# Picking table rows in quarters of 256 edges on 32 partitions instead of halves of 512 edges on 64

## The chip, the core and the metric

The kernel runs on one core of one Trainium2 chip. The core has TensorE (PE in the profile; its weight loads are shown apart as PEld), VectorE (DVE), ScalarE (ACT), GpSimd (POOL) and SyncE (SP), which issues most transfers. Each engine works through its own instructions in order and waits on semaphores of the others. The metric is the device time of one execution in microseconds, and the time of a kernel is the median of its runs.

## The reference

A graph layer with residual. There are 12500 nodes with 64 features and 212500 edges, sorted by `dst`; the inner layer calls `src` its `row` and `dst` its `col`.

```python
h = jnp.maximum(_layernorm(x, axis=-1), 0.0)
edge_in = jnp.concatenate([h[row], h[col], dist], axis=1)      # row = src, col = dst
e = jax.nn.silu(edge_in @ eW1 + eb1)                            # 129 -> 128
e = jax.nn.silu(e @ eW2 + eb2)                                  # 128 -> 128
agg = jax.ops.segment_sum(e, row, num_segments=h.shape[0])
node_in = jnp.concatenate([h, agg], axis=1)
out = jax.nn.silu(node_in @ nW1 + nb1) @ nW2 + nb2
x = x + out
```

The first product splits in three: `h[row] @ eW1[:64]`, `h[col] @ eW1[64:128]` and `dist * eW1[128]`. The kernel makes the first two per node and not per edge.

## The kernel before

Nodes are put in 100 buckets (node number modulo 100, 125 nodes each). Table `ta` holds `h @ eW1[:64]` and is used by `src`; table `tb` holds `h @ eW1[64:128]` and is used by `dst`. A short copy of the first rows of `tb`, called `tb0`, serves the first 30 blocks.

Work on edges has two parts, which are interleaved by hand.

**Sending.** The edges come in 208 blocks of 1024, two blocks to a pair, 104 pairs. For each edge the kernel makes the row `tb[dst] + dist * w1d + eb1` and writes it to a DRAM buffer `q`, at a place that belongs to the bucket of its `src`. Because the edges are sorted by `dst`, a stretch of 512 edges (a half) needs few rows of `tb`: 58 consecutive rows, the window, which SP loads into `win` (line 305). DVE compares the destinations, relative to the window, with the partition number and gets a one-hot matrix `pick` (line 338 for a pair, line 335 for a single block). Partitions 0 to 63 hold the first half of the block and 64 to 127 the second; in each, 58 rows are the one-hot, one holds the edge weights (SP writes it over, line 319) and one holds ones. `win` has the two windows on the same partitions, side by side in columns with zeros elsewhere, so one product of 128 partitions by 256 columns gives the rows of 128 edges of each half (line 389, four products to a block, each run by TensorE as two passes). ACT copies the products to `qs` (line 400) and adds the node's place (line 411). DVE counts each edge's rank in its bucket: a one-hot of the buckets (`oh`, line 339), a running sum along the edges in three pieces (line 350) and a product (line 356); TensorE picks the rank out (line 383) and DVE makes the address `to` (line 405). POOL then writes 128 rows at a time to `q` with an indirect transfer (line 418, eight to a block).

**Summing.** The 450 steps of the second part take four tiles of 128 rows of `q` each: find the node in the bucket (lines 494 and 499), add the row of `ta` (lines 508 and 514), silu (518), second product and silu (540, 546, 550), sum per node (527, 560), add to `aggT` (571). The node products (lines 232 to 244) follow for each four buckets at the end. Line 235 there is a product of 64 partitions, done twice, once for each half of the partitions.

The order on TensorE, VectorE, ScalarE and SP is the order of the Python program (`manual_schedule`). The list `turn` gives the order of a summing step; where it says `None`, pieces of the sending (three to a block) are put in, as many as the summing will need. A block is loaded two blocks ahead, and counted one block ahead, of its sending.

**The start.** POOL fills `zeros`, loads the weights, and copies the two rows `w1d` and `eb1` into the three `win` buffers, one small transfer for each row, column half and buffer (line 212), then fills three `xs` buffers (line 754). DVE fills the end of `srcR` (line 768), normalizes the first nodes (lines 587 to 599), computes the windows' first rows `lo` (lines 671 and 673), the relative destinations `rowsD` (675), and the buckets of the sources (692 to 695). SP loads the second part of `srcR` only after the fill of line 768. After that the first blocks are sent while the tables are made.

At the very end a flag tells whether every edge fitted its window and its places; if not, a general and slow branch does all sums again.

Of the kernel before, what the change touches and what calls it, by code (L numbers as in the profile page):

```python
# [40 lines left out]
WL = 58  # L41
STEP = 25
SPAN = 3 * STEP + WL
FEW = 12
HB = 64
BLK = 1024
HALF = BLK // 2
TB = BLK // P
PAIR = 2 * BLK
G = 4  # L50
# [22 lines left out]
def tile_gnn(ctx: ExitStack, tc: tile.TileContext, x, src, dst, ew, eW1, eb1, eW2, eb2, nW1, nb1, nW2, nb2, out):  # L73
# [10 lines left out]
    assert LEVELS[-1][1] == -(-E // BLK) and PAD < BLK and PAD % FEW == 0 and (-PAD) % HALF >= FEW  # L84
# [83 lines left out]
    nc.vector.tensor_scalar(plus, part, HB - 0.5, None, op0=OP.is_gt)  # L168
    nc.vector.scalar_tensor_tensor(same, plus, -float(HB), part, op0=OP.mult, op1=OP.add)
# [11 lines left out]
    dests = dram.tile([NP, 2, 2, HALF], BF16, name="dests")  # L181
    bucks = dram.tile([NP, 2, BLK], BF16, name="bucks")

    tb0 = dram.tile([P * NE, H], F32, name="tb0")
# [21 lines left out]
    for win in wins:  # L206
        nc.vector.memset(win, 0.0)
        for a in range(2):
            for i, row in enumerate((w1d, eb1b)):
                at = a * HB + WL + i  # L210
                for g in range(2):
                    nc.gpsimd.dma_start(win[at : at + 1, g, a, :], row[:1, :])
# [42 lines left out]
    with ExitStack() as work:  # L255
# [18 lines left out]
        def load_rows(s):  # L274

            if s < nblocks:
                p, g = s // 2, s % 2
                if g == 0:
                    bc = ld.tile([P, 2, HALF], BF16, name="bc")
                    bb = ld.tile([P, 2, BLK], BF16, name="bb")  # L280
                    lists[p] = [bc, bb, None]
                bc, bb, _ = lists[p]
                if g == 0 or p == 0:
                    m = 1 if p == 0 else 2
                    r, r2 = dests[p, 0, g], bucks[p, g]
                    of = bass.AP(tensor=r.tensor, offset=r.offset, ap=[[BLK, 2], [0, HB], [1, m * HALF]])
                    nc.sync.dma_start(bc[:, g : g + m].rearrange("p g e -> p (g e)"), of)
                    of = bass.AP(tensor=r2.tensor, offset=r2.offset, ap=[[0, 112], [1, m * BLK]])
                    nc.sync.dma_start(bb[:112, g : g + m].rearrange("p g e -> p (g e)"), of)
                blk[s] = [bc[:, g], bb[:, g]]  # L290

        def load(s):

            if s < nblocks:
                p, g = s // 2, s % 2
                win = wins[p % NW]
                table, end = (tb0, NE * P) if s < EARLY else (tb, NB * P)
                assert s < EARLY or len(done_b) == NB // G
                if g == 0:
                    at = nc.sync.value_load(base_i[:, p : p + 1], min_val=0, max_val=end - SPAN)  # L300
                    for a in range(2):
                        rows = table[bass.ds(at, SPAN), :]
                        of = [[H, WL], [2 * STEP * H, 2], [1, H]]
                        of = bass.AP(tensor=rows.tensor, offset=rows.offset + a * STEP * H, ap=of)
                        nc.sync.dma_start(win[a * HB : a * HB + WL, :, a, :], of)
                    lists[p][2] = ld.tile([P, 2, HALF], F32, name="pick")
                blk[s] += [win[:, g], lists[p][2][:, g]]
            load_rows(s + 1)

        def weights(s):  # L310

            if s < nblocks:
                p, g = s // 2, s % 2
                pick = lists[p][2][:, g]
                e0 = s * BLK
                m = 1 if p == 0 or e0 + 2 * BLK > E else 2
                if m == 2 or e0 + BLK <= E:
                    of = bass.AP(tensor=ew.tensor, offset=ew.offset + e0, ap=[[HALF, 2], [BLK, m], [1, HALF]])
                    nc.sync.dma_start(lists[p][2][WL::HB, g : g + m, :], of)
                else:  # L320
                    for a in range(2):
                        m = min(HALF, E - e0 - a * HALF)
                        if m > 0:
                            of = bass.AP(tensor=ew.tensor, offset=ew.offset + e0 + a * HALF, ap=[[m, 1], [1, m]])
                            nc.sync.dma_start(pick[a * HB + WL : a * HB + WL + 1, :m], of)
# [49 lines left out]
        def send(s):  # L375
# [10 lines left out]
            two = [2 if G + t < nt else 1 for t in range(min(G, nt))]  # L386
            qps = [mm.tile([P, 2, 2, H], F32, name="qp", tag="mm") for _ in range(2)]
            for t, k in enumerate(two):
                nc.tensor.matmul(  # L389
                    qps[t // 2][:, t % 2, :k], pick[:, t * P : (t + 1) * P], win[:, :k], start=True, stop=True  # L390
                )
            parts = []
            for i, qp in enumerate(qps):
                qs = qsp.tile([P, 2, 2, W], F32, name="qs")
                mine = [(t, k) for t, k in enumerate(two) if t // 2 == i]
                same = [(slice(0, 2), 2)] if mine == [(2 * i, 2), (2 * i + 1, 2)] else [
                    (slice(t % 2, t % 2 + 1), k) for t, k in mine
                ]
                for ts, k in same:
                    nc.scalar.copy(qs[:, ts, :k, :H], qp[:, ts, :k, :])  # L400
                parts.append((i, same, qs))
            for i, same, qs in parts:
# [5 lines left out]
                places = locE[:, g * TB : (g + 1) * TB, p].rearrange("p (a i t) -> p i t a", a=2, i=2)  # L408
# [3 lines left out]
                for a in range(2):  # L412
                    for t in range(2 * i, 2 * i + 2):
                        j = a * G + t
                        if j >= nt:
# [5 lines left out]
                            in_=qs[:k, t % 2, a, :],  # L421
# [191 lines left out]
        def first_rows(g):  # L613
# [6 lines left out]
            nc.scalar.dma_start(tb0.rearrange("(p j) f -> p j f", j=NE)[:, g : g + G, :], got)  # L620
# [43 lines left out]
        def destinations():  # L664

            nc.scalar.copy(f, dstR)
            lim = lp.tile([NP, 1], F32, name="lim")
            nc.vector.tensor_scalar(lim, part[:NP], EARLY / 2 - 0.5, float((NB - NE) * P), op0=OP.is_gt, op1=OP.mult)
            nc.vector.tensor_scalar(lim, lim, float(NE * P - SPAN), None, op0=OP.add)
            yield  # L670
            nc.vector.tensor_scalar(lo[:, 0:1], fv[:, 0, 0:1], lim, None, op0=OP.min)
            for h in range(1, 4):
                nc.vector.tensor_scalar(lo[:, h : h + 1], lo[:, 0:1], float(h * STEP), None, op0=OP.add)
            for g in range(2):
                nc.vector.tensor_tensor(
                    rowsD[:, :, g, :],
                    fv[:, 2 * g : 2 * g + 2, :],
                    lo[:, 2 * g : 2 * g + 2, None].to_broadcast([NP, 2, HALF]),
                    op=OP.subtract,
                )  # L680
            nc.sync.dma_start(dests, rowsD)
            yield
            lot = mm.tile([1, NP], F32, name="lot", tag="mm")
            nc.tensor.transpose(lot, lo[:, 0:1], ident[:NP, :NP])
# [37 lines left out]
        def checks():  # L722

            ends = lp.tile([NP, 2, 4], F32, name="ends")
# [33 lines left out]
        with tc.tile_pool(name="lists", bufs=1, side="right") as lp:  # L758
# [5 lines left out]
            fv = f.rearrange("p (g e) -> p g e", e=HALF)  # L764
            lo = lp.tile([NP, 4], F32, name="lo")
            rowsD = lp.tile([NP, 2, 2, HALF], BF16, name="rowsD")
# [228 lines left out]
```

## Time and profile before

| | |
|---|---|
| median of 6 runs | 3200.42 us (3171.43 to 3207.57) |
| profiled execution | 3207.37 us, span 3205.6 us |
| PE busy | 2454.3 us (77%) |
| PEld busy | 2176.4 us (68%) |
| DVE busy | 1888.7 us (59%) |
| ACT busy | 1097.1 us (34%) |
| POOL busy | 1726.7 us (54%) |
| mean granted clock of TensorE | 0.859 |
| moved by the DMA engines | 495.01 MB |

In a group line of the profile stand the line of the kernel, the engine, the operation, what it writes and reads, the shapes, the count, then busy time and mean length of one in ns, then the engine's idle time just before and what ended it. A matmul's record runs on past the start of the next one, so the mean of one is longer than the distance between two. A timeline line has the start in us, the length of the merged stretch in us, the engine, the line, the operation and the count; "idle before" and what ended it stand in brackets. A line of windows has the stretch, its length, then the busy time (and count) of each engine, the granted clock, the DMA share and GB/s.

### The profile page before, as it was taken

The page shows a single profiled execution, that of the slowest core. Times are in us where ns is not written, and L with a number is a line of the kernel's source. Part 1 is how long each engine was busy: PE and PEld are TensorE (multiplying, and loading weights), DVE is VectorE, ACT ScalarE, POOL GpSimd, SP SyncE. Part 2 cuts the span into 40 slices and gives each one's busy share as a digit, 9 for nine tenths or more (in the row PEclk, how much of TensorE's full clock was granted, in tenths as well). Part 3 has the DMA queues.
Part 4 walks back from the last instruction along what each step waited for, and adds up shares of the span by engine and source line. Part 5 has one row for each costly group of instructions (what it writes and reads, how often), then busy time and mean ns, then how long its engine had stood idle before and what let it go on. Part 6 is the DMA issues. An engine that isn't in the chain of part 4 may idle for free. (4 is left out here: it accounts for less than half of the span.)

```text
span 3205.6 us, 48057 instructions
## 1 busy us (share of the span) xinstructions
PE 2454.3 (77%) x17253; PEld 2176.4 (68%) x17253; DVE 1888.7 (59%) x3129; ACT 1097.1 (34%) x2410; POOL 1726.7 (54%) x1737
## 2 busy tenths in 40 slices
PE   3563576655788888888888788878878888888998
PEld 2442465554677777777777777767767777788987
DVE  6554565655665656666566666666666666665433
ACT  3331232222233333333333333333333333344443
POOL 4566655666656656555565656556555555543000
PEclk9666777777798888898888989899899989899999
DMA  4553355555566656544444444444344444555441
GB/s 120 182 173 128 118 158 175 182 170 166 186 193 195 204 186 199 175 152 147 137 134 150 134 146 153 138 147 154 128 149 144 151 143 125 165 168 168 139 141 56
DMA packets 230686, 495.01 MB, mean 154 GB/s; under 512 B 43137, under 2 KB 85106, under 8 KB 230235
## 3 DMA queue, kind: packets, MB, share of 16 engines
q1 hardware_dynamic: 155454, 324.52, 32.5%
q0 software_dynamic: 54400, 123.05, 11.0%
q10 hardware_dynamic: 20586, 44.30, 4.7%
q8 instruction: 139, 2.28, 0.3%
q14 instruction: 107, 0.87, 0.1%
HBM read 305.41 MB, written 186.28 MB: 153 GB/s over the span
## 5 line engine op out<-in xcount | busy, mean ns | idle before, releaser
L418 POOL DMA_INDIRECT q<-qs,to x1661 | 1681.7, 1012 | 1230.2 <-ACT qs L411 674.8
L350 DVE TENSOR_TENSOR_SCAN misc<-oh,misc 100x342 f32<-100x342 f16 (+1 forms) x617 | 575.5, 933 | 207.3 <-remote 123.1
L518 ACT ACTIVATE e<-pt 128x512 f32<-128x512 f32 x450 | 270.6, 601 | 1205.3 <-remote 428.8
L560 PE MATMUL seg<-one,e 128*128 128x125 f32 x3600 | 547.8, 293 | 137.1 <-issue 95.9
L499 DVE TENSOR_SCALAR oneT<-lr,part 125x512 f32<-125x512 f32 x450 | 336.1, 747 | 472.2 <-remote 184.0
L560 PEld LDWEIGHTS seg<-one,e 128*128 128x128 f32 x3600 | 492.3, 207 | 155.9 <-issue 135.2
L546 PE MATMUL p<-w,e 128*128 128x128 f32 x3600 | 543.2, 294 | 51.4 <-issue 44.2
L546 PEld LDWEIGHTS p<-w,e 128*128 128x128 f32 x3600 | 509.6, 207 | 100.0 <-issue 66.5
L514 PE MATMUL pt<-oneT,a 125*128 125x256 f32 (+1 forms) x2200 | 532.8, 373 | 31.5 <-issue 30.4
L389 PE MATMUL qp<-win,pick 128*128 128x256 f32 x1664 | 491.0, 441 | 62.0 <-issue 42.3
L389 PEld LDWEIGHTS qp<-win,pick 128*128 128x128 f32 x1664 | 356.6, 224 | 134.3 <-issue 71.2
L514 PEld LDWEIGHTS pt<-oneT,a 125*128 125x128 f32 x2200 | 378.5, 212 | 66.0 <-issue 41.3
L571 DVE TENSOR_TENSOR aggT<-aggT,seg 128x500 f32<-128x500 f32 x250 | 168.0, 672 | 402.4 <-remote 140.9
L400 ACT COPY qs<-qp 128x512 f32<-128x512 f32 x418 | 233.4, 587 | 441.0 <-PE qp L389 108.5
L550 ACT ACTIVATE e<-p 128x512 f32<-128x512 f32 x450 | 271.2, 603 | 280.5 <-PE pt L514 67.7
L508 PE MATMUL pt<-ident,qt 128*128 128x128 f32 x1800 | 308.3, 296 | 61.6 <-ACT e L518 34.7
L356 DVE TENSOR_TENSOR own<-misc,oh 100x342 f16<-100x342 f32 (+1 forms) x623 | 319.5, 513 | 21.5
L527 DVE TENSOR_TENSOR one<-nodes,qt 128x500 f32<-128x500 f32 x450 | 301.4, 670 | 0.5 <-PE seg L560 0.5
L494 PE MATMUL lr<-identb,qt 128*125 128x128 bf16 x1800 | 202.4, 232 | 97.2 <-issue 68.0
L508 PEld LDWEIGHTS pt<-ident,qt 128*128 128x128 f32 x1800 | 214.3, 152 | 82.5 <-ACT e L518 42.6
L540 ACT COPY p<-b2f 128x512 f32<-128x512 f32 x450 | 269.3, 598 | 0.1
L494 PEld LDWEIGHTS <-qt 128*125 128x125 bf16 x1800 | 177.8, 146 | 119.5 <-issue 107.1
(120 smaller groups left out, 981.4 us busy)
## 6 DMA issues: line engine op xcount, KB each, us to landing
qt<-q SPq DMA_DIRECT2D x175, 576.0 KB
a<-ta SPq DMA_DIRECT2D x275, 256.0 KB
bb<-bucks SPq DMA_DIRECT2D x103, 448.0 KB
qt<-q SPq DMA_DIRECT2D x100, 288.0 KB
q<-qs,to POOLq DMA_INDIRECT x1661
bc<-dests SPq DMA_DIRECT2D x103, 256.0 KB
q<-zeros ACTq DMA_DIRECT2D x20, 1080.0 KB
q<-zeros ACTq DMA_DIRECT2D x10, 1440.0 KB
```

The costliest lines, as they stand in the source:

```text
L350: nc.vector.tensor_tensor_scan(run[:, :m], oh[:, cols], nil.to_broadcast([NB, m]), carry[-1] if carry else -1.0 - MID, op0=OP.add, op1=OP.add)
L356: nc.vector.tensor_tensor(own[:, cols], run[:, :m], oh[:, cols], op=OP.mult)
L389: nc.tensor.matmul(qps[t // 2][:, t % 2, :k], pick[:, t * P : (t + 1) * P], win[:, :k], start=True, stop=True)
L418: ins = nc.gpsimd.indirect_dma_start(out=q[:], out_offset=bass.IndirectOffsetOnAxis(ap=to[:k, j : j + 1], axis=0), in_=qs[:k, t % 2, a, :] ...
L494: nc.tensor.matmul(lr[:L, t, :], loc[:, at : at + 1].to_broadcast([P, L]), identb, start=True, stop=True)
L499: nc.vector.tensor_scalar(oneT, st[k].pop("lr")[:L], part1[:L, :], None, op0=OP.is_equal)
L508: nc.tensor.matmul(pt[:, t, :], qt[:, j, :H], ident, is_transpose=True, start=t == 0, stop=False, skip_group_check=True)
L514: nc.tensor.matmul(pt[:, cols, :], a[:L, b, :], oneT[:, cols, :], start=False, stop=True, skip_group_check=True)
L527: nc.vector.tensor_tensor(one.rearrange("p (b j) l -> p b j l", j=n), nodes1[:, None, None, :].to_broadcast(wide), loc[:, tiles[0][1] : ti ...
L546: nc.tensor.matmul(p2[:, t, :], e1[:, t, :], w2, start=False, stop=t == G - 1, skip_group_check=True)
L550: nc.scalar.activation(e2, p2, AF.Silu)
L560: nc.tensor.matmul(item[2][:, b, :], e2[:, t, :], one[:, t, :], start=j < G, stop=j >= G * (n - 1))
```

## The change

A block is divided in quarters of 256 edges instead of halves of 512. A quarter has 32 partitions: 30 rows of `tb`, one weight row, one row of ones. The four windows of a block start 15 rows apart. `pick` becomes 128 by 256 for a block, where it was 128 by 512. The product takes 64 partitions (two quarters, side by side in 256 columns as the halves were) and alternates between partitions 0 to 63 and 64 to 127; there are still four products to a block, of the same 256 columns. `win` is loaded by four transfers of 30 rows for each of two blocks, where there were two of 58. The eight tiles of a block are numbered so that a quarter is two tiles.

The windows' common start of a pair becomes the least over its eight quarters of first destination minus offset, bounded below; so that a window may start before row 0, `tb0` gets 16 rows of zeros in front. The offsets (0, 15, ..., 105) come from a new iota on POOL, `steps_i`, which DVE copies to `steps15`; in the program these stand just before the fill of `srcR`. The small transfers of `w1d` and `eb1` into the `win` buffers become 48, from 24. The counts by running sums along the edges, which the change's title names, are the same in both kernels.

```diff
-WL = 58
-STEP = 25
-SPAN = 3 * STEP + WL
+WL = 30
+STEP = 15
+SPAN = 7 * STEP + WL
+FRONT = 16
...
-HB = 64
+NQR = 4
...
-HALF = BLK // 2
+QR = BLK // NQR
...
-    tb0 = dram.tile([P * NE, H], F32, name="tb0")
+    tb0 = dram.tile([FRONT + P * NE, H], F32, name="tb0")
+    nc.gpsimd.dma_start(tb0[:FRONT], zeros[:FRONT, :H])
...
-        for a in range(2):
+        for a in range(NQR):
             for i, row in enumerate((w1d, eb1b)):
-                at = a * HB + WL + i
+                at = a * 32 + WL + i
                 for g in range(2):
-                    nc.gpsimd.dma_start(win[at : at + 1, g, a, :], row[:1, :])
+                    nc.gpsimd.dma_start(win[at : at + 1, g, a % 2, :], row[:1, :])
...
-                    of = bass.AP(tensor=r.tensor, offset=r.offset, ap=[[BLK, 2], [0, HB], [1, m * HALF]])
+                    of = bass.AP(tensor=r.tensor, offset=r.offset, ap=[[2 * QR, NQR], [0, 32], [1, m * QR]])
...
-                    for a in range(2):
-                        rows = table[bass.ds(at, SPAN), :]
-                        of = [[H, WL], [2 * STEP * H, 2], [1, H]]
+                    for a in range(NQR):
+                        rows = table[bass.ds(at - front, SPAN), :]
+                        of = [[H, WL], [NQR * STEP * H, 2], [1, H]]
                         of = bass.AP(tensor=rows.tensor, offset=rows.offset + a * STEP * H, ap=of)
-                        nc.sync.dma_start(win[a * HB : a * HB + WL, :, a, :], of)
-                    lists[p][2] = ld.tile([P, 2, HALF], F32, name="pick")
+                        nc.sync.dma_start(win[a * 32 : a * 32 + WL, :, a % 2, :], of)
+                    lists[p][2] = ld.tile([P, 2, QR], F32, name="pick")
...
-            two = [2 if G + t < nt else 1 for t in range(min(G, nt))]
+            halves = [[sum(4 * i + 2 * a + t < nt for a in range(2)) for t in range(2)] for i in range(2)]
             qps = [mm.tile([P, 2, 2, H], F32, name="qp", tag="mm") for _ in range(2)]
-            for t, k in enumerate(two):
-                nc.tensor.matmul(
-                    qps[t // 2][:, t % 2, :k], pick[:, t * P : (t + 1) * P], win[:, :k], start=True, stop=True
-                )
+            for t in range(2):
+                for i, n_of in enumerate(halves):
+                    if n_of[t]:
+                        at = slice(64 * i, 64 * i + 64)
+                        nc.tensor.matmul(
+                            qps[i][:, t, : n_of[t]], pick[at, t * P : (t + 1) * P], win[at, : n_of[t]], start=True, stop=True
+                        )
...
+            far = lp.tile([NP, 1], F32, name="far")
+            for h in range(-(-LAST // QR), 2 * NQR):
+                nc.vector.tensor_scalar(far, part[:NP], NP - 1.5, float(BEYOND), op0=OP.is_gt, op1=OP.mult)
+                assert h == 2 * NQR - 1
+                nc.vector.tensor_scalar(fv[:, h, :], fv[:, h, :], far, None, op0=OP.add)
...
-            nc.vector.tensor_scalar(lo[:, 0:1], fv[:, 0, 0:1], lim, None, op0=OP.min)
-            for h in range(1, 4):
-                nc.vector.tensor_scalar(lo[:, h : h + 1], lo[:, 0:1], float(h * STEP), None, op0=OP.add)
+            base = lp.tile([NP, 1], F32, name="base")
+            nc.vector.tensor_tensor(lo, fv[:, :, 0], steps15[:NP], op=OP.subtract)
+            nc.vector.tensor_reduce(base, lo, AX.X, OP.min)
+            nc.vector.tensor_scalar(base, base, lim, low, op0=OP.min, op1=OP.max)
+            nc.vector.tensor_scalar(lo, steps15[:NP], base, None, op0=OP.add)
...
+            steps15 = lp.tile([P, 2 * NQR], F32, name="steps15")
+            steps_i = lp.tile([P, 2 * NQR], I32, name="steps_i")
+            nc.gpsimd.iota(steps_i, pattern=[[STEP, 2 * NQR]], base=0, channel_multiplier=0)
+            nc.vector.tensor_copy(steps15, steps_i)
```

## The prediction

> **What bounds the kernel now.** I read the totals first, then the work by stage, then TensorE's own order around the product that the change touches, and last the start. The page: its first line, TensorE's busy tenths and its granted clock.
>
> ```profile
> PE 2454.3 (77%) x17253; PEld 2176.4 (68%) x17253; DVE 1888.7 (59%) x3129; ACT 1097.1 (34%) x2410; POOL 1726.7 (54%) x1737
> ...
> PE   3563576655788888888888788878878888888998
> ...
> PEclk9666777777798888898888989899899989899999
> ```
>
> TensorE is the fullest engine from about 800 us on (eight to nine tenths), and its clock there is near full. Before that it is half idle and slow. The same by stage, for line 389 alone (the product that changes):
>
> ```profile
> 0.00:340.00 340.00, 79.01 (x184) 52.93 (x184) 0.72 0.47 147
> 340.00:800.00 460.00, 88.22 (x280) 63.48 (x280) 0.74 0.53 165
> 800.00:2945.00 2145.00, 323.80 (x1200) 240.23 (x1200) 0.89 0.49 157
> ```
>
> Eight passes are a block: 23, 35 and 150 blocks. What TensorE waited for between 800 and 2800 us:
>
> ```profile
> PE misc L383 <- DVE own L356: 54.7, 34, 3.3
> PE seg L560 <- issue: 46.6, 67, 5.7
> ...
> PE seg L560 <- DVE aggT L571: 29.3, 26, 2.8
> ```
>
> These are small against 2000 us, so TensorE's own work sets most of the pace there. How one block stands in TensorE's timeline, and the only products on 64 partitions in the summing loop, those of line 235:
>
> ```profile
> 2002.06 1.06 PE L546 MATMUL p<-w,e 128*128 128x128 f32 x8
> 2002.95 1.89 PE L389 MATMUL qp<-win,pick 128*128 128x256 f32 x8
> 2004.68 1.05 PE L560 MATMUL seg<-one,e 128*128 128x125 f32 x8
> ```
>
> ```profile
> 2980.93 1.01 PE L232 MATMUL z<-aggT,w1g 128*128 128x250 f32 x4
> 2981.88 0.69 PE L235 MATMUL z<-hrn,w1n 64*128 64x250 f32 x4
> 2982.50 1.16 PE L546 MATMUL p<-w,e 128*128 128x128 f32 x8
> 2983.49 0.77 PE L241 MATMUL o<-w2n,zs 128*125 128x64 f32 x6
> ```
>
> Read the distances between starts. Line 389: 2004.68 - 2002.95 = 1.73 us for 8 passes, 0.216 each. Line 235: 0.62 us for 4 passes of 250 columns, where line 232 needs 0.95 for 4 passes of the same columns: the two halves overlap. The start, on POOL and DVE:
>
> ```profile
> 18.29 0.98 POOL L212 DMA_DIRECT2D win<-w1d  x2
> ...
> 22.12 2.41 POOL L212 DMA_DIRECT2D win<-w1d  x2
> ...
> 31.98 2.11 POOL L754 MEMSET xs<- 128x768 f32 x3
> ```
>
> ```profile
> 10.03 1.22 DVE L587 TENSOR_REDUCE mean<-x 128x16 f32<-128x1024 f32 x1 [6.71 <-DMA x<-in_x_dram]
> ...
> 19.23 0.21 DVE L671 TENSOR_SCALAR lo<-f,lim 104x1 f32<-104x1 f32 x1 [2.17 <-ACT f L666]
> ...
> 21.94 1.23 DVE L692 TENSOR_SCALAR t<-sf 104x2048 f32<-104x2048 f32 x1
> ```
>
> DVE starts on the nodes at 10 us; POOL is done with its small transfers and fills at 34 us and nobody waits for that.
>
> **The change part by part.** The sum is made against the profiled execution, 3207.4 us; the median shown is 7.0 lower, and I take that off at the end.
>
> *The products.* A pass of 250 columns costs 0.216 x 250/256 = 0.211. From line 232 to 235: 0.95 - 4 x 0.211 = 0.105 too much; line 235 to 546: 0.62 - 2 x 0.211 = 0.20 too much if two passes run side by side; after it line 546 takes 0.99 where an undisturbed one takes 0.89 (2002.06 to 2002.95), 0.10 too much. So a change to 64 partitions and back costs 0.405 us, and the passes in between run in pairs. A block then takes 4 x 0.216 + 0.405 = 1.27 instead of 1.73: 0.46 less at full clock. Over the run: the busy time has an overhang of 1.89 - 1.73 = 0.16 a block. For 340 to 800 us, 88.2 - 35 x 0.16 = 82.6, half is 41.3. At half clock the switch lies between 0.405 and 0.81; at a mean clock of 0.74 I take 0.50, 35 x 0.50 = 17.5, net 23.8. For 800 to 2945 us, 323.8 - 24.0 = 299.8, half 149.9, switches at clock 0.89 150 x 0.45 = 67.5, net 82.4. How much of this reaches the end? TensorE is busy 82% of the late stage and its waits for others are under a tenth; I take three quarters, 62 us. In the earlier stage (busy 63%, half clock much of the time) 0.55, 13 us. Ends: a quarter of both (27) and all (106). Before 340 us TensorE is half idle: 0 to 10, I take 3.
>
> The Trainium skill bears on this twice. "TensorE: Matmul & The Clock Gate", Part 3, gives a pack of row tiles the time of one matmul plus about 4 ns for each further tile; by that alone the gain of TensorE would be 41.3 + 149.9 = 191 us. "TensorEngine Tiling (Array Packing)", Key Properties, speaks against it: a change of tiling mode drains TensorE. The 0.405 us of the rows agrees with the second, and the sum goes by the rows.
>
> *The pick.* A pair's comparison shrinks from 128x1024 to 128x512:
>
> ```profile
> L338 DVE TENSOR_SCALAR pick<-bc,same,plus 128x1024 f32<-128x1024 bf16 x102 | 82.6, 809 | 0.0
> ...
> L335 DVE TENSOR_SCALAR pick<-bc,same,plus 128x512 f32<-128x512 bf16 x4 | 2.2, 544 | 9.0 <-DMA bc<-dests 9.0
> ```
>
> 102 x (0.809 - 0.544) = 27 us of DVE, which is idle two fifths of the time and mostly waits for TensorE. I take a tenth, 3 us; ends 0 and 14.
>
> *The start.* In the built order of the changed kernel the iota of the offsets stands on POOL behind 48 small transfers and the three fills, and DVE's copy of it stands ahead of the fill of `srcR` and of the first reduction over the nodes. So DVE, and behind it all of the start, waits for POOL. POOL reaches the first small transfer at 18.3 + 0.5 (the zeros of `tb0`). 48 at 0.48 (0.98 for two) end at 41.8; with the slower ones (13.7 us for 24 before) at 46.2. Fills 2.1, iota 0.2 (the length of line 136's): 44 to 48.5. Then copy and fill 0.7, reduction at 45 instead of 10.0: +35. Destinations were late before (DVE stood 2.17 us for `f`); that wait is gone, but the new step on `f` stands before the node's last two operations (1.5 us), and seven small DVE operations of about 0.15 replace four. I get line 692's successor at about 58 instead of 21.9, +36. SP's second part of `srcR` also starts only then, and ACT needs it seven us later; if it is late, up to 5 more. Two more window loads before the first product add 0.7. I take +37, ends 34 and 45. Everything after hangs on this chain, so it is paid in full.
>
> *SP.* 206 more window loads at 0.37 (the one at 2000.16 us) are 76 us of issue; SP stands 921 us waiting for DVE at line 469 between 800 and 2800, and a window is loaded two blocks ahead. Without that cover it would be 0.7 us a pair. The destinations' broadcast halves, about 13 of 495 MB. Both zero, ends 0 and +10. The 8 indirect transfers, the copies and the counts of a block stay.
>
> *The clock.* It is 0.74 where TensorE is 63% busy and 0.89 where it is 82%. Less work on TensorE takes it from 82% to about 80%: by that slope 0.015 of clock, 20 us or so; since it is work and not waiting that goes away, I take 10; ends 0 and 23.
>
> Sum: 3207.4 + 37 - 62 - 13 - 3 - 3 + 10 = 3173, less 7.0: 3166 us.
>
> **The rivals.**
> 1. *The loop keeps little.* TensorE arrives earlier only to stand at lines 383, 560 or 494, for the scans of DVE or for the "issue" waits that no engine ends. For: POOL (1228.8 us) and DVE (1339.8 us) work 8 to 9 us a block between 800 and 2945, out of 14; against: most DVE waits end on TensorE. At a third, 35 us with the rest: 3207 + 37 - 35 - 7 = 3202.
> 2. *The other side: the halves do not overlap.* Passes would follow each other, and the switches come on top: 85 us of TensorE, three quarters of it 64. 3207 + 37 + 64 - 7 = 3301. It decides as soon as a block takes more than its old 1.73 us. Against it: the 0.62 us of line 235.
> 3. *All of it reaches the end*, the clock holds: with 10 us from before 340 us and 5 from DVE, 3207 + 36 - 106 - 10 - 5 - 7 = 3115.
> That the windows of 30 are too narrow and the general branch runs, I rule out: counted over the reference's edge list, no destination lies more than 21 rows after its window's start.
>
> **How the numbers follow.** Forecast 0.50 (3145 to 3190), rival 1 0.22, rival 2 0.10, rival 3 0.18. The range 3115 to 3230 leaves out rival 2 and the low edge of rival 3. Half a per cent, 16 us, is about what the runs can tell. Faster (below 3184): 0.45 of the forecast, 0.03 of rival 1, all 0.18 of rival 3, 0.66. Same: 0.04 and 0.12, 0.16. Slower: 0.01, 0.07 and 0.10, 0.18.
>
> **What would show it.** The start: DVE's reduction over the first nodes at 43 to 48 us, ended by POOL. The product: eight passes with 1.2 to 1.3 us from first start to the next line's start, the records in pairs. The late stage: the same number of blocks in some 60 us less, clock 0.87 or more. I am wrong if a block still takes 1.7 us, if POOL's small transfers do not hold DVE, or if TensorE's idle time from 800 us on grows by as much as its work shrinks.

## The result, and the profile after

The changed kernel takes 3233.88 us (median of 20 runs, 3210.61 to 3256.62) where the kernel before takes 3201.81 (46 runs): a ratio of 1.0113, 95% interval 1.0093 to 1.0134. By the ratio it is about 36 us slower; the medians differ by 32 us. The profiled execution took 3235.39 us, with a span of 3233.6. All ratios here are over fast runs alone, so they need not be the quotient of the two medians, and the microseconds given with a ratio are the ratio's.

First the page: the totals, TensorE's busy tenths and its granted clock.

```profile
PE 2419.2 (75%) x17251; PEld 2070.9 (64%) x17251; DVE 1868.2 (58%) x3136; ACT 1088.4 (34%) x2406; POOL 1732.5 (54%) x1763
...
PE   1454377566588778778787888788788888888998
...
PEclk9655577666788888888988888899888988989999
```

TensorE has 35 us less busy time than before, and this execution's span is 28 us longer. The mean clock is 0.835, where it was 0.859. Only the first slices of the PE row differ plainly from before: the start is emptier.

The start, DVE in the timeline (start and length in us, in brackets the idle time before and what ended it):

```profile
41.76 0.17 DVE L786 CAST steps<-steps_i 128x8 f32<-128x8 int32 x1 [37.66 <-POOL steps_i L785]
42.08 0.47 DVE L789 MEMSET srcR<- 8x492 int32 x1
42.58 1.22 DVE L594 TENSOR_REDUCE mean<-x 128x16 f32<-128x1024 f32 x1
...
55.23 1.22 DVE L709 TENSOR_SCALAR t<-sf 104x2048 f32<-104x2048 f32 x1
```

DVE waits 37.66 us for POOL, whose iota follows the 48 small transfers. The line that makes `t` (692 before, 709 now) starts at 55.23 us instead of 21.94: +33.3. The 48 end at 39.5 us: none of them is slow as two pairs of before were.

The product, in TensorE's timeline:

```profile
2001.09 1.05 PE L567 MATMUL seg<-one,e 128*128 128x125 f32 x8
2002.07 1.13 PE L397 MATMUL qp<-win,pick 64*128 64x256 f32 x8
2003.14 0.44 PE L501 MATMUL lr<-identb,qt 128*125 128x128 bf16 x4
```

Eight passes now take 2003.14 - 2002.07 = 1.07 us, where they took 1.73. The line behind them is longer too, as these rows of the changed kernel in its later run on another chip show:

```profile
1503.96 1.14 PE L397 MATMUL qp<-win,pick 64*128 64x256 f32 x8
1505.03 1.16 PE L553 MATMUL p<-w,e 128*128 128x128 f32 x8
1506.02 1.05 PE L567 MATMUL seg<-one,e 128*128 128x125 f32 x8
```

Line 553 takes 1506.02 - 1505.03 = 0.99 us here, where line 546 took 0.89 undisturbed (2002.06 to 2002.95 in the prediction's rows). In the records at full clock lines 553 and 567 take 0.10 us more right behind the product than elsewhere, and lines 501 and 515 take 0.05.

Line 397 alone by stage (length, busy time and count of PE, then of PEld, clock, DMA share, GB/s):

```profile
340.00:800.00 460.00, 64.29 (x272) 35.37 (x272) 0.69 0.50 156
800.00:2945.00 2145.00, 216.31 (x1216) 123.37 (x1216) 0.88 0.48 154
```

Its busy time fell by 107.5 us in the late stage, with two blocks more in it. Now all engines in that stage, before and then after (PE, PEld, DVE, ACT, POOL):

```profile
800.00:2945.00 2145.00, 1753.30 (x12512) 1577.51 (x12512) 1339.78 (x2215) 772.79 (x1668) 1228.84 (x1209) 0.89 0.49 157
```

```profile
800.00:2945.00 2145.00, 1725.27 (x12431) 1488.09 (x12428) 1330.26 (x2225) 762.59 (x1657) 1238.24 (x1222) 0.88 0.48 154
```

Here is the whole case: 107.5 us left the product, but TensorE's busy time fell by only 28.0, for nearly the same work (12431 matmuls, 12512 before). The other 79.5 us came back in the other products, which became longer. Groups of the whole run show it, before and then after:

```profile
L560 PE MATMUL seg<-one,e 128*128 128x125 f32 x3600 | 547.8, 293 | 137.1 <-issue 95.9
...
L546 PE MATMUL p<-w,e 128*128 128x128 f32 x3600 | 543.2, 294 | 51.4 <-issue 44.2
```

```profile
L567 PE MATMUL seg<-one,e 128*128 128x125 f32 x3600 | 567.2, 301 | 128.9 <-issue 74.9
L553 PE MATMUL p<-w,e 128*128 128x128 f32 x3600 | 580.8, 304 | 97.1 <-issue 85.1
```

Lines that the change does not touch got 19.4 and 37.6 us longer (in the late stage alone 7.1 and 24.5), and one of them waits 45.7 us more. Lined up by block, POOL's first write of a block is late by 30.9 us in block 0, 33.0 in block 20, 51.1 in block 101, 32.6 in block 188 and 32.4 in block 206; the last step ends 33.3 us later. What follows the last step is 5.3 us shorter, for which no reason is shown. In this pair of executions the loop as a whole kept nothing, and the loss is the start. One pair settles that only roughly: executions of the kernel before differ by up to 58 us (3171.43 to 3229.45), and the lateness swings by some 19 us within this one. The experiments have to show it.

### The profile page after: what moved, and what is told of

Same layout as the page of the kernel before. It is cut to its first block, busy times and chain, and to the rows that moved or that the text cites. A ratio compares the mean times of both kernels' runs of the same rounds, so it can differ in the third digit from the quotient of the medians.

```text
span 3233.6 us, 48796 instructions
## 1 busy us (share of the span) xinstructions
PE 2419.2 (75%) x17251; PEld 2070.9 (64%) x17251; DVE 1868.2 (58%) x3136; ACT 1088.4 (34%) x2406; POOL 1732.5 (54%) x1763
## 2 busy tenths in 40 slices
DMA packets 238983, 481.91 MB, mean 149 GB/s; under 512 B 50165, under 2 KB 106996, under 8 KB 238526
## 3 DMA queue, kind: packets, MB, share of 16 engines
q0 software_dynamic: 55200, 123.07, 10.7%
## 5 line engine op out<-in xcount | busy, mean ns | idle before, releaser
L567 PE MATMUL seg<-one,e 128*128 128x125 f32 x3600 | 567.2, 301 | 128.9 <-issue 74.9
L553 PE MATMUL p<-w,e 128*128 128x128 f32 x3600 | 580.8, 304 | 97.1 <-issue 85.1
L553 PEld LDWEIGHTS p<-w,e 128*128 128x128 f32 x3600 | 530.9, 215 | 167.7 <-issue 128.2
L567 PEld LDWEIGHTS seg<-one,e 128*128 128x128 f32 x3600 | 502.7, 212 | 171.8 <-issue 147.9
L521 PE MATMUL pt<-oneT,a 125*128 125x256 f32 (+1 forms) x2200 | 549.5, 382 | 33.9 <-issue 32.9
L521 PEld LDWEIGHTS pt<-oneT,a 125*128 125x128 f32 x2200 | 391.1, 220 | 70.6 <-issue 45.8
L397 PE MATMUL qp<-win,pick 64*128 64x256 f32 x1662 | 328.3, 469 | 70.9 <-issue 54.0
L515 PE MATMUL pt<-ident,qt 128*128 128x128 f32 x1800 | 321.5, 305 | 70.0 <-ACT e L525 31.9
L407 ACT COPY qs<-qp 128x512 f32<-128x512 f32 x416 | 225.0, 590 | 392.5 <-remote 145.9
L397 PEld LDWEIGHTS qp<-win,pick 64*128 64x128 f32 x1662 | 187.5, 219 | 143.9 <-issue 107.1
```

What stands on the lines that cost most here:

```text
L397: nc.tensor.matmul(qps[i][:, t, : n_of[t]], pick[at, t * P : (t + 1) * P], win[at, : n_of[t]], start=True, stop=True)
L515: nc.tensor.matmul(pt[:, t, :], qt[:, j, :H], ident, is_transpose=True, start=t == 0, stop=False, skip_group_check=True)
L521: nc.tensor.matmul(pt[:, cols, :], a[:L, b, :], oneT[:, cols, :], start=False, stop=True, skip_group_check=True)
L553: nc.tensor.matmul(p2[:, t, :], e1[:, t, :], w2, start=False, stop=t == G - 1, skip_group_check=True)
L567: nc.tensor.matmul(item[2][:, b, :], e2[:, t, :], one[:, t, :], start=j < G, stop=j >= G * (n - 1))
```

## The experiments

No profile says how much of TensorE's work is on the path, so the runs change one thing each, most of them on the kernel before. The chips matter. On one chip (first group) the kernel before takes 3176 us (median), near the 3202 of the comparison; on three others it takes 2574 to 2578 us. I call these the slow and the quick chips. Each ratio is against the kernel before on the same chip.

### On a slow chip: the start and the product

**The offsets ahead** (changed kernel, the iota and its copy beside the constants, so that neither queue holds DVE):

```diff
     nc.vector.tensor_copy(nodes1, nodes_i)
+    steps_i = const.tile([P, 2 * NQR], I32, name="steps_i")
+    nc.gpsimd.iota(steps_i, pattern=[[STEP, 2 * NQR]], base=0, channel_multiplier=0)
+    steps15 = const.tile([P, 2 * NQR], F32, name="steps15")
+    nc.vector.tensor_copy(steps15, steps_i)
...
-            steps15 = lp.tile([P, 2 * NQR], F32, name="steps15")
-            steps_i = lp.tile([P, 2 * NQR], I32, name="steps_i")
-            nc.gpsimd.iota(steps_i, pattern=[[STEP, 2 * NQR]], base=0, channel_multiplier=0)
-            nc.vector.tensor_copy(steps15, steps_i)
```

> The changed kernel with the iota of the window offsets and its copy on DVE set beside the other constants, ahead of all small transfers; nothing else. Theory A (the start is the whole of the loss, the loop is as long as before): DVE's first reduction over the nodes comes back to about 10 us and the time falls by the 33 us of the start, to about 3200, a ratio of 1.00. Theory B (the loop itself also got slower, or the late start hides a gain): 3215 or more, or below 3185.

Measured: 3167.85 us against 3175.57, ratio 0.9961 (0.9925 to 0.9998). The 48 small transfers are still there; the line that makes `t` starts at 23.9 us. The loss is gone with the place of two instructions. What the shorter products are then worth is small: 12 us (1 to 24) by the ratio, 8 by the medians. The changed kernel as it was did not run on this chip.

**The late start alone** (kernel before, small transfers doubled, an iota and its copy before the fill of `srcR`):

```diff
-                    nc.gpsimd.dma_start(win[at : at + 1, g, a, :], row[:1, :])
+                    for _ in range(2):
+                        nc.gpsimd.dma_start(win[at : at + 1, g, a, :], row[:1, :])
...
+            late_i = lp.tile([P, 8], I32, name="late_i")
+            nc.gpsimd.iota(late_i, pattern=[[15, 8]], base=0, channel_multiplier=0)
+            late = lp.tile([P, 8], F32, name="late")
+            nc.vector.tensor_copy(late, late_i)
```

> The kernel before with each small transfer of w1d and eb1 made twice, and an iota behind them that DVE copies ahead of the fill of srcR; products, windows and lists as before. Theory A: +33 us, about 3235, the same as the changed kernel. Theory B: another value, since part of the changed kernel's loss then lies in its loop.

Measured: 3207.33 us, ratio 1.0084 (1.0054 to 1.0115), 27 us slower (17 to 36; the medians differ by 32), with the `t` line at 54.1 us, 32 later than the 21.94 of the profile before. The start is paid nearly in full. This run and the last stand on one chip: the `t` line of the last is 30.2 us earlier and its median 39.5 us lower, which leaves some 9 us for the shorter products.

**Half of the product** (kernel before, 128 columns at line 389; the rows of the second half of a block are left out, the copies repeat those of the first):

```diff
-                    qps[t // 2][:, t % 2, :k], pick[:, t * P : (t + 1) * P], win[:, :k], start=True, stop=True
+                    qps[t // 2][:, t % 2, :1], pick[:, t * P : (t + 1) * P], win[:, :1], start=True, stop=True
...
-                    nc.scalar.copy(qs[:, ts, :k, :H], qp[:, ts, :k, :])
+                    n_t = ts.stop - ts.start
+                    nc.scalar.copy(qs[:, ts, :k, :H], qp[:, ts, :1, :].to_broadcast([P, n_t, k, H]))
```

> The kernel before with 128 columns in the product of line 389 where there were 256 (the rows of the second half of each block are left out and those of the first stand in their place): 128 partitions, no change of array mode, the same copies. Theory A1 (TensorE's work at this line does not set the loop's pace, however it is shortened): within 15 us of 3202. Theory A2 (shorter products do help; the products on 64 partitions lose their gain to the changes of mode and the clock): 0.86 us x 185 blocks x 0.75 = 120 us less, about 3080, at least 60 less.

Measured: 3147.24 us, ratio 0.9895 (0.983 to 0.9959): 33 us (13 to 54). Eight passes take 0.90 us where undisturbed (0.113 each, before 0.216), so 1664 passes are some 170 us less work for TensorE. About a fifth of it arrives (8 to 32%); that lies between the two theories, nearer to the first.

**The product twice** (kernel before):

```diff
+                for _ in range(2):
                     nc.tensor.matmul(
```

> The kernel before with each product of line 389 made twice: 1.73 us more of TensorE's work in a block at full clock. Theory A1 (the product has slack): under 80 us more, 3202 to 3280. Theory A2 (TensorE sets the pace): 1.73 x 185 x 0.75 = 240 us more, about 3440.

Measured: 3197.67 us, ratio 1.0033 (0.9993 to 1.0072): 10 us (-2 to 23) for 1664 x 0.216 = 359 us more work; the medians differ by 22. Its windows and, under them, those of the kernel before for the same stretch (in the execution of the comparison):

```profile
800.00:2000.00 1200.00, 1065.30 (x7580) 958.41 (x7580) 754.37 (x1250) 429.67 (x932) 723.62 (x707) 0.95 0.53 168
```

```profile
800.00:2000.00 1200.00, 974.69 (x6771) 871.16 (x6771) 751.83 (x1244) 426.48 (x925) 705.85 (x696) 0.88 0.52 166
```

The added work fills time in which TensorE stood, and the clock rises from 0.88 to 0.95 (over the whole run from 0.864, the mean of the runs of the kernel before on this chip, to 0.917), so each product is quicker: line 546's group has a mean of 297 ns before and 284 ns here. In this stretch the doubled line is busy 152.8 us more (340.7, before 187.9) and TensorE as a whole 90.6; the other 62.2 us are what the other lines lost. POOL writes at the same pace (707 and 696). So work added to TensorE is nearly free in this loop, and of work taken away about a fifth arrives. This refutes the three quarters of my prediction more directly than the change itself, where a slower start and an altered product come together. It doesn't tell how much the idle time paid for and how much the clock, since both moved.

### On quick chips: which engine sets the pace

On the second chip the kernel before takes 2577.16 us. There each run doubles one leg of the kernel before.

```diff
             nc.vector.tensor_scalar(oh, bb[:NB, :], part[:NB, :], None, op0=OP.is_equal)
+            nc.vector.tensor_scalar(oh, bb[:NB, :], part[:NB, :], None, op0=OP.is_equal)
```

> The kernel before with the one-hot of the buckets (line 339, 0.49 us on DVE) made twice in each block: 208 x 0.49 = 102 us more on DVE, ahead of the scans. Theory D (DVE's order sets the loop's pace): 70 to 110 us more. Theory P (POOL's writes set it) and theory W (no engine alone, a ring of waits): under 40 us.

Measured: 2579.22 us, ratio 1.0006 (0.9989 to 1.0023).

```diff
                     nc.scalar.copy(qs[:, ts, :k, :H], qp[:, ts, :k, :])
+                    nc.scalar.copy(qs[:, ts, :k, :H], qp[:, ts, :k, :])
```

> The kernel before with both copies of the products to qs (line 400) made twice: 2 x 0.59 x 208 = 245 us more on ACT, which stands between the product and POOL's writes and also holds two of TensorE's four output buffers that much longer. Theory E (what the loop waits for is the way through ACT, not TensorE's passes): 120 us more or above. Theories D and P: under 60 us.

Measured: 2580.87 us, ratio 1.0009 (0.9988 to 1.003).

```diff
+    spent = const.tile([P, 2, H], F32, name="spent")
...
+                if same == [(slice(0, 2), 2)]:
+                    nc.gpsimd.tensor_tensor(spent, qs[:, 0, :, :H], qs[:, 1, :, :H], op=OP.add)
```

> The kernel before with two additions of 128x256 on POOL (0.77 us each by line 220's row) in each block, ahead of its indirect writes: 320 us more on POOL. Theory P: 200 us more or above. Theories D and E: under 80 us, since POOL stands idle 44% of the span.

Measured: 2864.14 us, ratio 1.1105 (1.1072 to 1.1139), 285 us of the 320 added.

```diff
-                nc.tensor.matmul(lr[:L, t, :], loc[:, at : at + 1].to_broadcast([P, L]), identb, start=True, stop=True)
+                for _ in range(2):
+                    nc.tensor.matmul(lr[:L, t, :], loc[:, at : at + 1].to_broadcast([P, L]), identb, start=True, stop=True)
```

> The kernel before with the four products of line 494 made twice in each of the 450 steps: 450 x 0.25 = 110 us more of TensorE's work, at another place than line 389. If TensorE's work has slack at any place: under 30 us more and a higher granted clock. If only the product of line 389 has slack: 80 us more or above.

Measured: 2588.08 us, ratio 1.0028 (1.0014 to 1.0042): 7 us (4 to 11) of 110, at a mean clock of 0.941, before 0.932.

Of these four only POOL's work arrives on this chip. It is full: POOL's groups between 800 and 2000 us, first in the kernel before on a slow chip, then on a quick one (in the kernel with ACT's copy doubled, which costs nothing there and stands in for the kernel before; columns: busy time, mean ns, idle time before and what ended it):

```profile
L418 POOL DMA_INDIRECT q<-qs,to x696 | 707.2, 1016 | 494.5 <-ACT qs L411 281.6 <-issue 181.2 <-ACT p L540 10.3
```

```profile
L419 POOL DMA_INDIRECT q<-qs,to x900 | 923.6, 1026 | 277.8 <-issue 219.8 <-DMA q<-qs,to 12.1 <-ACT p L541 7.9
```

On the quick chip a write follows the last after about 0.3 us of its own issue: 1200 / 900 = 1.33 us a write, 10.7 us a block. On the slow chip the same writes wait 281.6 us for ACT, whose copy at line 400 waits most for TensorE's product (107.6 of its 440.2 us over the run): 1.72 us a write, 13.8 a block.

Now the changed kernel itself on such a chip, with three more legs.

> The changed kernel once more, beside the kernel before on one chip. Theory T (the loop's pace is not set by TensorE's work, so the shorter product is given back as waiting, and only the start remains): 25 to 40 us slower than before on whichever chip it runs, that of 3200 us as that of 2577 us, since the late first block (+33 us in the trace) is the whole difference. Theory P (the product is on the path, and the loss of the first comparison came from something else in the change, a longer matmul elsewhere or the clock): on a chip where TensorE has no issue gaps (before at 2577 us) the product's gain shows and the kernel is 0 to 60 us faster.

Measured: 2557.24 us against 2576.05, ratio 0.9927 (0.9896 to 0.9959): **faster** by 19 us, with the same late start. Theory T falls as a statement on all chips. Of theory P the numbers for such a chip hold, where TensorE has no issue gaps and the product's gain shows; that the first loss came from another part of the change than the start does not. Aligned by block with the profile of the doubled copy on the same chip, it is 29.7 us late at block 2, 19.0 at block 188, and 11.6 us early at block 206. Between blocks 2 and 188, where POOL is full, the loop gains 10.7 us; over the last 18 blocks 30.6. The last step ends 12.3 us early and the execution 17.4.

> The kernel before with two additions of 128x256 on POOL in each block (+320 us of POOL's work), as in the run that cost 287 us on a chip where before takes 2577 us. POOL sets the pace of the loop everywhere: 250 to 320 us slower again. POOL sets it only where TensorE is not held up: on a chip where before takes about 3200 us, whose POOL waits 753 us for ACT in the profile, it costs under 80 us; on a chip of 2577 us again 287.

Measured: 2857.81 us, ratio 1.1098 (1.106 to 1.1137). The chip was again a quick one: 283 us, after 285.

> The kernel before with ACT's copy of the product made twice (+245 us of ACT's work), which cost nothing on a chip where before takes 2577 us. If ACT's copies stand in the ring that sets the pace on a chip of about 3200 us (POOL waits 675 us for them there), 80 to 245 us slower; if the ring has room, under 20 us, as before.

Measured: 2577.57 us, ratio 1.0016 (0.9996 to 1.0036). Nothing again.

```diff
-            nc.vector.tensor_scalar(oneT, st[k].pop("lr")[:L], part1[:L, :], None, op0=OP.is_equal)
+            lr = st[k].pop("lr")
+            for _ in range(2):
+                nc.vector.tensor_scalar(oneT, lr[:L], part1[:L, :], None, op0=OP.is_equal)
```

> The kernel before with DVE's one-hot of places in each step made twice (450 x 0.747 = +336 us of DVE's work, in the ring lr to oneT to pt). If DVE's chain sets the pace, 150 to 336 us slower; if TensorE's own supply of instructions or POOL sets it, under 40 us.

Measured: 2625.21 us, ratio 1.0192 (1.0157 to 1.0227): 49 us of 336, between the two numbers. DVE is then busy 1128 of 1200 us between 800 and 2000, so it has become nearly as full as POOL.

**The changed kernel with its offsets ahead, on a quick chip** (the kernel of the first experiment):

> The changed kernel with the step table's iota and copy ahead of the small transfers (its first block at the old time), beside the kernel before. Theory T: on a chip where before takes 2576 us, TensorE gets its instructions without gaps, and the loop's and the tail's gain of 43 us stands without the late start: 40 to 55 us faster than before (ratio 0.979 to 0.985). On a chip of 3200 us, 0 to 25 us faster, as in the first look (ratio 0.996). Rival: the late start is hidden on the chip of 2576 us, since POOL sets the pace there: 15 to 25 us faster, as the changed kernel itself was.

Measured: 2529.15 us against 2573.79, ratio 0.9825 (0.9798 to 0.9853), 45 us faster (38 to 52). As expected: the 19 us of the change with its late start, and 26 for the start on top (from two quick chips). This version is faster than the kernel before on both kinds of chip, on the slow one by no more than the interval shows (1 to 24 us).

**Fewer of TensorE's instructions** (kernel before, one of four products of places):

```diff
-            for t, (j, _) in enumerate(tiles):
+            for t, (j, _) in enumerate(tiles[:1]):
...
-            nc.vector.tensor_scalar(oneT, st[k].pop("lr")[:L], part1[:L, :], None, op0=OP.is_equal)
+            nc.vector.tensor_scalar(oneT, st[k].pop("lr")[:L, 0:1].to_broadcast([L, G, P]), part1[:L, :], None, op0=OP.is_equal)
```

> The kernel before with one of the four products of places in a step (line 494) and the other three left out: 1350 of 17253 matmuls fewer, 150 to 160 us of TensorE's work, and the one-hot of places made from the first product for all four tiles, so three quarters of the edges get wrong places. Supply theory (on a chip of 3200 us the number of instructions that TensorE takes sets the loop): 150 to 250 us faster there. Ring theory (TensorE's work is one leg among several, and what is taken from it goes to waits and half clock): under 50 us faster there, as with the halved product (33 us). On a chip of 2576 us, where POOL sets the pace: under 30 us faster.

Measured: 2571.39 us, ratio 0.9986 (0.997 to 1.0002). On a quick chip it brings 4 us (0 to 8), as POOL sets the pace; the question for a slow chip was not answered. The 150 to 160 us were read from the records' busy time; by the distance between starts (0.23 to 0.26 us for the four products) the work left out is an estimated 78 to 88 us.

**One addition on POOL for each block**, the kernel with more of POOL's work, under the condition `i == 0 and`:

> The kernel before with one addition of 128x256 on POOL in each block (208 x 0.73 to 0.77 us = +155 us of POOL's work). Where POOL sets the pace (before 2576 us): 120 to 160 us slower. Where before takes 3200 us: under 40 us slower if POOL has room there, 120 to 160 if POOL's writes set the pace there too and their waits for ACT are only their order.

Measured: 2713.09 us, ratio 1.0551 (1.0517 to 1.0585): 142 us of 155.

These two once more:

> The addition of 128x256 on POOL in each block (+155 us of POOL's work) once more. It cost 139 us on a chip where before takes 2574 us, and does so again on another such chip (130 to 145). On a chip where before takes about 3200 us: under 40 us if POOL has room there, 120 to 160 us if POOL's writes set the pace there too.

> 1350 of TensorE's matmuls left out once more (three of four products of places, so three quarters of the edges get wrong places). It brought 2 us on a chip where before takes 2574 us, and under 10 us on another such chip. On a chip where before takes about 3200 us: 150 to 250 us faster if the number of TensorE's instructions sets the pace there, under 50 us if what is taken from TensorE goes to waits and half clock, as with the halved product (33 us).

It was a quick chip again, that of the second group (2578.47 us). Measured: 2711.37 us, ratio 1.0522 (1.0489 to 1.0554), and 2568.09 us, ratio 0.997 (0.9951 to 0.9989). Both are nearly as on the other quick chip: 135 us slower, and 8 us faster (3 to 13).

### What remains open on the slow chips

TensorE has stretches there in which its instructions come slowly, without a wait that the trace shows. The kernel before, TensorE's timeline:

```profile
2431.12 0.58 PE L383 MATMUL misc<-fours,own 100*128 100x1 f16 x6
2432.18 0.16 PE L383 MATMUL misc<-fours,own 100*128 100x1 f16 x1 [0.48 <-issue]
2432.91 0.17 PE L383 MATMUL misc<-fours,own 100*128 100x1 f16 x1 [0.56 <-issue]
2432.94 0.36 PE L560 MATMUL seg<-one,e 128*128 128x125 f32 x1
2434.32 0.49 PE L560 MATMUL seg<-one,e 128*128 128x125 f32 x3 [1.02 <-issue]
...
2440.19 0.27 PE L494 MATMUL lr<-identb,qt 128*125 128x128 bf16 x1 [1.25 <-issue]
2440.91 0.35 PE L494 MATMUL lr<-identb,qt 128*125 128x128 bf16 x1 [0.46 <-issue]
2441.63 0.27 PE L494 MATMUL lr<-identb,qt 128*125 128x128 bf16 x1 [0.36 <-issue]
```

Matmuls that otherwise follow each other in 0.03 to 0.11 us come 0.7 us apart, or twice that. I counted in the records of each run how often, after 330 us, two successive matmuls of one line start more than 0.55 us apart:

```
kernel, chip                       intervals   sum us   mean clock
before, slow                          342        354      0.859
changed, slow                         433        423      0.835
half of the product, slow             390        401      0.829
changed, offsets ahead, slow          449        428      0.843
late start alone, slow                363        336      0.872
product twice, slow                   288        290      0.916
before with copy twice, quick          11          6      0.934
changed, quick                         19         11      0.927
```

So the three kernels with a shorter product meet more of this (401 to 428 us) than the two with the old one (336 and 354), and the doubled one less (290). The changed kernel has 69 us more than before. The product's busy time after 340 us fell by 131.4 us (88.22 - 64.29 and 323.80 - 216.31), so about half of that would come back in this shape. This is a correlation. What the stretches are is not shown; they stand at all distances from the transfers of TensorE's instructions, and of the 342 of the kernel before only 27 fall on the same matmul in the late start alone. Half clock doesn't explain them either: 55% of those before lie wholly in time at full clock. The plain number of TensorE's instructions does not set the pace on a slow chip: the doubled product has 1664 matmuls and as many weight loads more, and cost 10 us (22 by the medians). Whether more work on POOL, DVE or ACT would arrive there, the runs can't say, since every run that tests them was made on a quick chip.

## Why the prediction was wrong, point by point

- **The failed step is "How much of this reaches the end? ... I take three quarters, 62 us"**, and with it the 0.55 for 340 to 800 us (13 us). On the chip of the comparison it was about zero: the aligned blocks show 33 us late at block 20 and 32.4 at block 206. On the slow chip of the first group the changed kernel without its late start gains 12 us (1 to 24), and halving the old product 33. The reason given for it, TensorE busy 82% and its waits for others under a tenth, read too much out of busy time. Records of matmuls run past the next start, and the same products take longer at half clock: the eight passes of line 546 take 0.89 us where the clock is 1.0 and 1.71 where it is 0.5. By the distances between starts around 2000 us at full clock (0.26, 0.44, 0.87, 0.89 and 0.89 us for lines 494, 508, 514, 546 and 560, 1.73 and 0.20 a block for lines 389 and 383) the 354 steps and 150 blocks of the late stage are an estimated 1475 us of work, 69% of its 2145 and not 82%. Doubling the product at +10 us shows how much room there was. Small waits of TensorE did not make it the bound: the late stage has no full engine (POOL 57%, DVE 62%). What does set the pace on a slow chip, and so why the shorter product comes back as longer products (79.5 us) and idle time (28.0), stays open. My sign for being wrong, idle time that grows by as much as the work shrinks, would have missed most of it.
- **"The lower end of the range"**: I had a quarter as the least of what arrives, "ends: a quarter of both (27) and all (106)". That excluded zero without a reason, and about zero is what came. Even so the measured 3233.88 lies 4 us above the range's upper end. Worked with my own sum, nothing kept and the start as measured gives 3207.4 + 33.3 - 7.0 = 3233.7 us. That it fits so closely is luck, since half a per cent is 16 us.
- **Rival 1 (the loop keeps little) is what happened**, and it named the "issue" waits that no engine ends, but at the wrong lines. Between 800 and 2800 us they grew at line 546 (34.3 to 56.4 us) and fell at lines 383, 560 and 494 (28.7 to 24.3, 46.6 to 34.5, 46.2 to 42.3). Its price assumed a third kept. I ranked it at 0.22, against it that most waits of DVE end on TensorE; that only says that TensorE is a leg of the ring, not that its work is the length of it.
- **The product: right, and better than predicted.** I had 1.27 us for a block from a switch of 0.405, of which 0.10 stood for the longer line behind. The eight passes take 1.07 us to the next line's start, and that next line is longer too, by 0.05 to 0.10 us. So a block costs 1.12 to 1.17 us, and taking 4 x 0.216 for the passes in pairs, the switch into and out of 64 partitions costs 0.25 to 0.31. The Trainium skill's "TensorE: Matmul & The Clock Gate", Part 3, would have the pack of passes, as an estimate, at about 4 x 0.216 + 0.02; "TensorEngine Tiling (Array Packing)", Key Properties, has the drain, and the rows show 0.25 to 0.31 us beyond the passes. Rival 2 (no overlap) is refuted by the same rows.
- **The start: the mechanism right, the size a little high.** Predicted +37 (34 to 45), with the reduction at 43 to 48 us ended by POOL. Measured: reduction at 42.58 behind a copy that POOL ends, +33.3 at the `t` line. The term is 4 us too large, since POOL came to its first small transfer at 16.61 us and not at 18.8, and the slower transfers of before did not come back. By the late start alone it is worth 27 us (17 to 36) in time.
- **The clock: right for the late stage, too small for the run.** I took 0.015 of the late stage's clock, for 10 us (0 to 23); there it fell from 0.89 to 0.88. Over the run it fell by 0.024, since the stages ahead fell more (0.74 to 0.69 between 340 and 800 us, 0.72 to 0.66 before that, with the emptier start in it). I had argued that work and not waiting goes away, but waiting took part of the work's place. What the clock cost in time the runs don't separate. In the records of the clock between 340 and 2900 us, 237 of 750 granted windows were at half, before 205.
- **The pick**: 102 x 0.543 = 55.4 us, 27 less on DVE as predicted. Nothing of it shows in the loop's time, where I took 3.
- **SP and the transfers**: 13.1 MB less moved (481.91, before 495.01), as predicted, and SP still stands 887.7 us between 800 and 2800 us waiting for DVE at the line that loads `qt` (before 921.2). No run tests the further window loads alone.
- **Rival 3 (all reaches the end)** is refuted on both kinds of chip: with the offsets ahead a slow chip gains 12 us, and a quick one 45, where the product's busy time falls by 189.5 (463.2 with the one-hot doubled, which costs nothing there, and 273.7 in the changed kernel).

## What to carry to other kernels

Where no engine is full for a stage, work taken off the busiest one has no price until a run gives it: let "nothing arrives" be one end of the range, and test with the cheapest experiment, doubling the work in question. A new step that a first use waits for costs its whole place in the queue, so ask what stands ahead of it on the engine that makes it; here, on a slow chip, two instructions cost more than the products saved. And an edit can have opposite signs on two chips of one kind (1.0113 and 0.9927): on a quick chip POOL sets the pace of most blocks, and on a slow chip it is not known what does.

## What the runs showed of the hardware that I had not expected

- The same kernel takes 3176 and 3202 us (medians) in two groups of runs and 2574 to 2578 on three other chips. The mean clock of TensorE is about 0.86 in the former and 0.93 on the latter.
- More work for TensorE can make its other products quicker: with the product doubled the clock rises from 0.864 to 0.917, line 546's mean falls from 297 to 284 ns, and the time grows by 0.3%.
- Passes on 64 partitions that alternate between the halves overlap nearly fully: 1.07 us for eight of 256 columns, 1.73 on 128 partitions. The change of mode costs 0.25 to 0.31 us, of which 0.05 to 0.10 shows in the next line.
